# Layer 2's filler steps: from an even spread of a list to a fixed place in each attention unit

## The chip, the cores and the metric

The kernel runs on one core of one Trainium2 chip. The metric is the device time of one execution in microseconds (us); lower is better. A profile is one further execution, in which every instruction is recorded with its engine: TensorE (PE; its weight loads are PEld), VectorE (DVE), ScalarE (ACT), GpSimd (POOL) and SyncE (SP), which issues the DMAs.

## The reference

Four residual layers act in turn on an activation x of 4 images, 56 x 56 positions and 256 channels, all in float32:

```python
x = x + L0(_gn(x))   # 7x7 local attention, zero padded
x = x + L1(_gn(x))   # affinity over all 3136 positions of an image
x = x + L2(_gn(x))   # neighbourhood attention: 4 heads dense, 4 heads dilated by 2
x = x + L3(_gn(x))   # attention in shifted 7x7 windows
```

`_gn` normalises each group of 8 channels over the image. Only layer 2 is changed. It computes, per image,

```python
qkv = x @ w_qkv + b_qkv            # 256 -> 3 x 256, 8 heads of 32
attn = softmax(q @ k[window] + rpb)   # 7x7 window, clamped at the borders
out  = (attn @ v[window]) @ w_proj + b_proj
```

where heads 0 to 3 take their window with step 1 and heads 4 to 7 with step 2.

## The kernel before, in words

Channels lie on partitions (2 halves of 128), positions along the free dimension. Layer 2 goes through the images in chunks of 7 rows (392 positions, 32 chunks in all, numbered i), and attends in passes of 14 rows (16 passes, numbered r), in `stream`. One pass has 8 *units*, made by `pair(r, m, i)`: for each of four i first m = 0 (the dense heads) and then m = 1 (the dilated ones). So the even units, u0, u2, u4 and u6, are dense and the odd ones dilated.

`attend_pairs` runs over the units. For a unit it emits, in this order: the unit's logits (L1044, 32 matmuls into the PSUM tiles s0 and s1), the mask and exponentials (DVE L1051, ACT L1052 and L1054, POOL L1055), the sums of the two key pieces of the unit before (POOL L1064), the unit's *filler steps* (`w["fill"]`), then the products of the unit before (L1073, with v rows in `vp`, into ps_o), and its normalisation: a reciprocal (DVE L1598), a check sum of it (ACT L976, the tile `no`), and the multiply into the tile `attn` (DVE L1602, L1608).

The filler steps are other work of the layer that TensorE does between logits and products:

- `project_rows(i)` makes chunk i's values, keys and queries from its normalised rows `xn`, each in two halves, so six steps: v0, v1, k0, k1, q0, q1. A value step is 8 matmuls of 256 columns (L963) and a VectorE copy (L965). A key or query step is 4 matmuls of 392 columns (L946, in `project`) and ScalarE copies: four for keys (L1534; half 0 into kE and kI for the dense heads, half 1 into k2t for the dilated ones), one for queries (L1551). After v1 the values go to DRAM (L1529).
- `prepare(i)` normalises chunk i's rows on VectorE (L940) and then loads the chunk after it (L1493).
- `project_out(r - 1)` makes the output of the pass before: for each of two chunks two steps, here po0 to po3, each 4 matmuls (L946), the addition to the residual (DVE L1633) and its statistics (DVE L895). The first step of a chunk loads the residual (L1630), the second stores the result (L1636).
- `step_stats` does one of three steps that turn an image's statistics into the scale of the next normalisation, where one is pending: a VectorE aggregate, and two small matmuls, each followed by small VectorE (L914 to L918, L923) and GpSimd (L924, L926) instructions.

All projections write into two PSUM banks that take turns, `ps_m` (`m_bufs = 2`). v rows are gathered from DRAM when a unit's logits are emitted (L1592, tile `vp`, three buffers), by SP, whose queue runs in order.

Before, `stream` puts the pass's steps into one list (14 of chunks 2r + 3 and 2r + 4, with project_out after a quarter of it, and three statistics steps five places apart), and `spread` cuts that list into eight equal runs. For a full pass of 21 steps this gives, with ' for the second chunk:

| unit | steps |
|---|---|
| u0 | v0, v1 |
| u1 | k0, po0, po1 |
| u2 | po2, po3 |
| u3 | k1, statistics, q0 |
| u4 | q1, prepare, v0' |
| u5 | statistics, v1' |
| u6 | k0', k1', q0' |
| u7 | statistics, q1', prepare' |

Pass 0 has no output steps and no statistics steps, pass 14 one chunk only, pass 15 none. In layers 0 to 2 the framework's planner orders each engine's instructions: it goes by program order, but may take a later instruction that is ready first. In layer 3 the order is written out by hand. [...]two banks for ps_m, two for each of s0 and s1, two for ps_o.

Of the kernel before, what the change touches and what calls it, by code (L numbers as in the profile page):

```python
# [24 lines left out]
FP = mybir.dt.float32  # L25
# [10 lines left out]
P = 128  # L36
CC = C // P
# [59 lines left out]
WC2 = BT  # L97
# [734 lines left out]
def direct_blocks(ctx: ExitStack, tc: tile.TileContext, d: dict, watch):  # L832
# [7 lines left out]
    no_step = lambda: None  # L840
# [6 lines left out]
    def tokens_of(l, b, t0, n):  # L847
        return stream_of[l][b].rearrange("(h p) t -> p h t", p=P)[:, :, t0:t0 + n]
# [42 lines left out]
    def add_stats(l, b, i, x):  # L891

        if l < 4:
            for h in range(CC):
                nc.vector.bn_stats(out=raw[l][b][:, h, i, :], in_=x[:, h, :])  # L895
            seen_parts[l, b] = seen_parts.get((l, b), 0) + 1
            if seen_parts[l, b] == parts_of[l]:
                pending.extend(group_stats(l, b))
# [35 lines left out]
    def known(l, b):  # L934
        while (l, b) not in stats:
            pending.pop(0)()
        return stats[l, b]

    def normalise(dst, src, gst, h):
        nc.vector.tensor_scalar(dst, src, gst[:, h, 0:1], gst[:, h, 1:2], ALU.subtract, ALU.mult)  # L940

    def project(w, col, rhs, n):

        pm = ps_m()
        for h in range(CC):
            nc.tensor.matmul(pm[:, :n], lhsT=w[:, h, col:col + P], rhs=rhs(h),  # L946
                             start=(h == 0), stop=(h == CC - 1))
        return pm[:, :n]
# [144 lines left out]
    def spread(units, steps):  # L1093

        n = len(units)
        for i, w in enumerate(units):
            mine = steps[i * len(steps) // n:(i + 1) * len(steps) // n]
            w["fill"] = lambda mine=mine: [f() for f in mine]
            yield w

    def lazily(make, i, n):

        made = []
        return [lambda k=k: (made or made.extend(make(i)), made[k]()) for k in range(n)]
# [379 lines left out]
    def layer2(early, big, pool, brief):  # L1484
# [3 lines left out]
        xs, xns, q, attns = {}, {}, {}, {}  # L1488

        def load(i):  # L1490
            b, c = divmod(i, 2 * NSB)
            xs[i] = early.tile([P, CC, WC2], FP, tag="x", name="x2")
            nc.sync.dma_start(out=xs[i], in_=tokens_of(2, b, c * WC2, WC2))  # L1493
# [14 lines left out]
        def prepare(i):  # L1508
            b, c = divmod(i, 2 * NSB)
            x = xs.pop(i)  # L1510
            if i + 1 < NIMG * 2 * NSB:
                load(i + 1)
            xn = xns[i] = brief.tile([P, CC, WC2], FP, tag="xn", name="xn2")
            for h in range(CC):
                normalise(xn[:, h, :], x[:, h, :], known(2, b), h)
# [107 lines left out]
        def project_out(r):  # L1623
            b, g = divmod(r, NSB)

            def step(y, m, box={}):
                c = 2 * g + y
                if m == 0:
                    box["x"] = pool.tile([P, CC, WC2], FP, tag="xr", name="xr2")
                    nc.sync.dma_start(out=box["x"], in_=tokens_of(2, b, c * WC2, WC2))  # L1630
                x = box["x"]
                pm = project(w_p, m * P, lambda h: attns[r][:, h, y * WC2:(y + 1) * WC2], WC2)
                nc.vector.scalar_tensor_tensor(x[:, m, :], pm, bp2[:, m:m + 1], x[:, m, :], ALU.add, ALU.add)  # L1633
                if m:
                    add_stats(3, b, c, x)
                    nc.sync.dma_start(out=tokens_of(3, b, c * WC2, WC2), in_=x)  # L1636
            return [lambda m=m, y=y: step(y, m) for y in range(2) for m in range(CC)]

        def stream():
            n = NIMG * NSB  # L1640
            for r in range(n):
                steps = []
                for i in (2 * r + 3, 2 * r + 4):
                    if i < 2 * n:
                        steps += lazily(project_rows, i, 6)
                    if i + 1 < 2 * n:
                        steps.append(lambda i=i: prepare(i + 1))
                if r:
                    at = max(1, len(steps) // 4)
                    steps = steps or [no_step]  # L1650
                    steps[at:at] = project_out(r - 1)
                    for _ in range(3):
                        at = min(at + 5, len(steps))
                        steps.insert(at, step_stats)
                attns[r] = pool.tile([P, CC, 2 * WC2], FP, tag="attn", name="attn2")
                yield from spread([pair(r, m, i) for i in range(4) for m in range(2)], steps)

        prepare(0)
        for i in range(3):
            prepare(i + 1)  # L1660
            for step in project_rows(i):
                step()
        attend_pairs(pool, stream())
        for step in project_out(NIMG * NSB - 1):
            step()
# [304 lines left out]
```

## Time and profile before

| | |
|---|---|
| three runs | 4178.07, 4186.3, 4189.68 us |
| median | 4186.3 us |
| profiled execution | 4191.1 us from first to last instruction (4192.88 us device time) |
| busy, whole span | PE 95%, PEld 66%, DVE 57%, POOL 41%, ACT 32% |
| mean clock granted to TensorE | 0.975 |
| layer 2's passes | first logits at 2936.98 us, last output step ends near 3637 us |

In the page's rows by slice, each digit is a fortieth of the span (about 105 us) and gives the busy share in tenths, so that layer 2 is digits 28 to 34. In the list of waits, "A <- B" is the time in which engine and line A stood idle until B released it. In a timeline a line is a run of like instructions with its start and length, and in brackets the idle time before it.

### The profile page before, as it was taken

How to read it: one execution, taken by the hardware profiler on the slowest of the kernel's cores; microseconds unless marked ns; L12 is line 12 of the kernel's file. 1: busy time of each engine (PE TensorE's matmuls, PEld its weight loads, DVE VectorE, ACT ScalarE, POOL GpSimd, SP SyncE). 2: the span in 40 equal slices, each digit the busy share in tenths (PEclk: the TensorE clock that was granted, in tenths of full speed). 3: DMA queues.
4: the chain of work that ended last, by engine and by line, in shares of the span. 5: the costliest groups of instructions: out<-in, count | busy, mean ns of one | idle time of the engine just before them, and what ended most of it. 6: DMA issues, size and time to landing. Idle time of an engine off the chain costs nothing.

```text
span 4191.1 us, 92593 instructions
## 1 busy us (share of the span) xinstructions
PE 3978.8 (95%) x39191; PEld 2778.0 (66%) x39191; DVE 2380.0 (57%) x4437; ACT 1345.3 (32%) x2850; POOL 1738.4 (41%) x1883
## 2 busy tenths in 40 slices
PE   6899999799999999999999999998999999999998
PEld 4566666577777677776777767775666666666665
DVE  6777777633345433454334543445777777666665
ACT  2444445321111111121111111111554455444443
POOL 2566667611123211242112421123666666644444
PEclk9899999899999999999999999999999999999999
DMA  7344333310000100001000000001333343322221
GB/s 251 101 133 124 113 110 106 117 64 13 18 15 24 33 9 15 14 24 33 10 14 14 19 26 9 9 18 47 118 116 114 108 122 102 115 64 82 71 75 60
DMA packets 239794, 275.89 MB, mean 66 GB/s; under 512 B 22150, under 2 KB 231720, under 8 KB 238888
## 3 DMA queue, kind: packets, MB, share of 16 engines
q1 hardware_dynamic: 239082, 269.80, 20.7%
q8 instruction: 310, 5.08, 0.5%
q14 instruction: 114, 0.93, 0.1%
q10 hardware_dynamic: 288, 0.08, 0.0%
HBM read 190.29 MB, written 79.53 MB: 64 GB/s over the span
## 4 chain that ended last, share of the span: by engine, by line
PE 77%; DVE 12%; POOL 5%; issue 3%; ACT 2%; DMA 1%; SPq 0%; DVEq 0%; POOLq 0%; ACTq 0%
PE ps_m L946 15%; PE ps_o L1393 14%; PE ps_v L1385 11%; PE ps_s L1365 11%; PE ps_m L963 7%; PE ps_o L1073 5%; PE ps_s L1044 3%; PE ps_t L1380 3%; PE ps_o L1013 2%; DVE e L1051 2%; DVE rs L1598 1%; PE ps_s L998 1%; DVE rs L1218 1%; DVE xn L940 1%; PE ps_m L1329 1%
## 5 line engine op out<-in xcount | busy, mean ns | idle before, releaser
L1389 DVE TENSOR_TENSOR acc<-acc,ps_v 128x257 f32<-128x257 f32 x1104 | 459.5, 421 | 684.3 <-PE ps_v L1385 680.2
L1368 ACT ACTIVATE e<-ps_s 128x512 f32<-128x512 f32 (+3 forms) x364 | 200.7, 551 | 1465.9 <-PE ps_s L1365 1463.1
L1385 PE MATMUL ps_v<-xw,e 128*128 128x257 f32 x2400 | 638.8, 384 | 8.6 <-DVE acc L1389 8.6
L1393 PE MATMUL ps_o<-xw,at 128*128 128x257 f32 x2400 | 645.2, 391 | 0.5
L1365 PE MATMUL ps_s<-xnT,xd 128*128 128x512 f32 (+3 forms) x1456 | 630.2, 549 | 0.0
L1393 PEld LDWEIGHTS ps_o<-xw,at 128*128 128x128 f32 x2400 | 437.7, 190 | 131.7 <-ACT at L955 72.5
L1064 POOL TENSOR_TENSOR b<-e 126x336 f32<-126x336 f32 (+5 forms) x512 | 499.1, 995 | 15.7 <-ACT e L1052 7.5
L1385 PEld LDWEIGHTS ps_v<-xw,e 128*128 128x128 f32 x2400 | 423.8, 191 | 86.5 <-DVE acc L1389 27.8
L1361 POOL TENSOR_SCALAR xd<-xnT,vec 128x128 f32<-128x128 f32 x200 | 121.2, 617 | 786.9 <-PE ps_s L1365 780.5
L946 PE MATMUL ps_m<-xn,w_wqkv 128*128 128x392 f32 x1024 | 375.7, 505 | 25.8 <-ACT kE L1534 21.1
L1055 POOL TENSOR_TENSOR e<-e,m0t 126x672 f32<-126x672 f32 (+3 forms) x128 | 238.5, 1864 | 282.9 <-ACT e L1054 246.7
L1365 PEld LDWEIGHTS ps_s<-xnT,xd 128*128 128x128 f32 x1456 | 262.5, 190 | 139.8 <-issue 116.7
L1055 POOL TENSOR_TENSOR e<-e,bias 119x784 f32<-119x784 f32 (+5 forms) x128 | 244.2, 1908 | 236.5 <-ACT e L1054 236.1
L976 ACT ACTIVATE no<-rs 128x168 f32<-128x168 f32 (+2 forms) x256 | 93.8, 367 | 663.2 <-DVE rs L1598 323.9
L946 PEld LDWEIGHTS ps_m<-xn,w_wqkv 128*128 128x128 f32 x1024 | 186.4, 190 | 161.9 <-ACT kE L1534 31.0
L1073 PEld LDWEIGHTS ps_o<-e,vp 124*32 124x32 f32 (+3 forms) x8192 | 177.6, 111 | 138.0 <-issue 95.0
L1380 PEld LDWEIGHTS ps_t<-ident,e 128*128 128x128 f32 x1200 | 152.5, 142 | 143.9 <-issue 137.4
L1598 DVE RECIPROCAL rs<-ps_o 128x196 f32<-128x196 f32 (+2 forms) x128 | 176.3, 1377 | 124.6 <-PE ps_o L1073 124.5
L1073 PE MATMUL ps_o<-e,vp 124*32 124x112 f32 (+3 forms) x8192 | 240.4, 254 | 4.7 <-POOL e L1055 3.3
L963 PE MATMUL ps_m<-w_wqkv,xn 128*98 128x256 f32 x1024 | 243.6, 383 | 0.4 <-DVE xr L1440 0.4
L940 DVE TENSOR_SCALAR xn<-x,gst 128x28 f32<-128x28 f32 (+5 forms) x368 | 205.0, 612 | 40.8 <-PE ps_m L946 33.1
L1052 ACT ACTIVATE e<-e 126x672 f32<-126x672 f32 (+5 forms) x256 | 219.4, 857 | 25.3 <-DVE e L1051 11.8
(149 smaller groups left out, 6150.3 us busy)
## 6 DMA issues: line engine op xcount, KB each, us to landing
x<-xr SPq DMA_DIRECT2D x64, 392.0 KB
x<-in_x SPq DMA_DIRECT2D x53, 448.0 KB
x<-x SPq DMA_DIRECT2D x60, 392.0 KB
xr<-x SPq DMA_DIRECT2D x60, 392.0 KB
vd<-v SPq DMA_DIRECT2D x28, 448.0 KB
xr<-in_x SPq DMA_DIRECT2D x32, 392.0 KB
xr<-x SPq DMA_DIRECT2D x28, 448.0 KB
x<-xr SPq DMA_DIRECT2D x28, 448.0 KB
```

Of the source, the lines that this page charges most:

```text
L940: nc.vector.tensor_scalar(dst, src, gst[:, h, 0:1], gst[:, h, 1:2], ALU.subtract, ALU.mult)
L946: nc.tensor.matmul(pm[:, :n], lhsT=w[:, h, col:col + P], rhs=rhs(h), start=(h == 0), stop=(h == CC - 1))
L963: nc.tensor.matmul(pm[:n, j * C:(j + 1) * C], lhsT=xn[:, h, k * n:(k + 1) * n], rhs=w[:, h, :], start=(h == 0), stop=(h == CC - 1))
L1052: nc.scalar.activation(ev, ev, AF.Exp)
L1055: nc.gpsimd.tensor_tensor(parts(ev), parts(ev), w["emask"], ALU.mult)
L1064: nc.gpsimd.tensor_tensor(w["b"][a][:nk, :, :2 * nq].rearrange("p h (i c) -> p h i c", i=2), ev[:, :, :, 0, :], ev[:, :, :, 1, :], ALU.add)
L1073: nc.tensor.matmul(w["o"](k, i)[j * HD:(j + 1) * HD], lhsT=ones[:nk, :HD] if k else v(j, u), rhs=w["b"][j // 2][:nk, j % 2, i * nq:(i + 1) ...
L1365: nc.tensor.matmul(s[:, :n], lhsT=xd[j][:, h, :], rhs=xnT[:, h, first * P:last * P], start=(h == 0), stop=(h == CC - 1))
L1380: nc.tensor.transpose(pt[:, col(i)], e[:, col(i)], ident)
L1385: nc.tensor.matmul(pv[:, :C + 1], lhsT=e[:, col(i)], rhs=xw[:, j, :], start=True, stop=True)
L1389: nc.vector.tensor_tensor(acc[:, i, :], acc[:, i, :], pv[:, :C + 1], ALU.add)
L1393: nc.tensor.matmul(out[j][:, :C + 1], lhsT=e[:, col(i)] if i == j else at[:, col(i)], rhs=xw[:, i, :], start=(i == j), stop=(i == NB - 1))
```

## The change

Each unit of a pass is given its steps by number, in `work`, and `spread` is no longer used for this layer. For the two chunks (y = 0 and 1), unit 4y gets v0 and k0, unit 4y + 1 gets v1 and q0, unit 4y + 2 gets k1, unit 4y + 3 gets q1 and then the normalisation of the next chunk. The four output steps of the pass before go to the ends of u2, u3, u6 and u7, and the statistics steps to the ends of u1, u4 and u5 (in pass 0 too). The tile for the pass's result is taken before the steps are laid out.

| unit | steps |
|---|---|
| u0 | v0, k0 |
| u1 | v1, q0, statistics |
| u2 | k1, po0 |
| u3 | q1, prepare, po1 |
| u4 | v0', k0', statistics |
| u5 | v1', q0', statistics |
| u6 | k1', po2 |
| u7 | q1', prepare', po3 |

```diff
             for r in range(n):
-                steps = []
-                for i in (2 * r + 3, 2 * r + 4):
+                attns[r] = pool.tile([P, CC, 2 * WC2], FP, tag="attn", name="attn2")
+                work = [[] for _ in range(8)]
+                for y, i in enumerate((2 * r + 3, 2 * r + 4)):
                     if i < 2 * n:
-                        steps += lazily(project_rows, i, 6)
+                        v0, v1, k0, k1, q0, q1 = lazily(project_rows, i, 6)
+                        for a, steps in enumerate(((v0, k0), (v1, q0), (k1,), (q1,))):
+                            work[4 * y + a] += steps
                     if i + 1 < 2 * n:
-                        steps.append(lambda i=i: prepare(i + 1))
+                        work[4 * y + 3].append(lambda i=i: prepare(i + 1))
                 if r:
-                    at = max(1, len(steps) // 4)
-                    steps = steps or [no_step]
-                    steps[at:at] = project_out(r - 1)
-                    for _ in range(3):
-                        at = min(at + 5, len(steps))
-                        steps.insert(at, step_stats)
-                attns[r] = pool.tile([P, CC, 2 * WC2], FP, tag="attn", name="attn2")
-                yield from spread([pair(r, m, i) for i in range(4) for m in range(2)], steps)
+                    for u, step in zip((2, 3, 6, 7), project_out(r - 1)):
+                        work[u].append(step)
+                for u in (1, 4, 5):
+                    work[u].append(step_stats)
+                for u, w in enumerate(pair(r, m, i) for i in range(4) for m in range(2)):
+                    w["fill"] = lambda steps=work[u]: [f() for f in steps]
+                    yield w
```

## The prediction

> **What bounds the kernel now.** I read the page first: TensorE's busy share by slice, to see whether layer 2 (about 2937 to 3637 us) is limited by it.
>
> ```profile
> PE   6899999799999999999999999998999999999998
> PEclk9899999899999999999999999999999999999999
> ```
>
> TensorE is busy nine tenths or more of slices 28 to 34, at nearly full clock: what this layer can gain is TensorE's idle time. Next the waits between 2945 and 3600 us (total us, times, longest), which say what ended it:
>
> ```profile
> PE ps_m L946 <- ACT kE L1534: 33.1, 25, 3.0
> PE ps_m L946 <- DVE v L965: 4.7, 5, 3.2
> PE ps_s L1044 <- DVE e L1051: 0.8, 1, 0.8
> ```
>
> Nearly all of it is one wait: a projection's matmuls want one of the two ps_m banks while ScalarE (L1534, the copies of a key projection) or VectorE (L965, values) still empties it. 37.8 us in all. I then cut one pass of `stream` (r = 6) at the starts of its eight units' logits; columns are TensorE busy (matmuls), clock, DMA share, GB/s:
>
> ```profile
> 3204.68:3210.52 5.84, 5.84 (x101) 1.00 0.25 71
> 3210.52:3218.17 7.65, 6.72 (x97) 1.00 0.45 141
> 3218.17:3223.20 5.03, 5.03 (x92) 1.00 0.52 153
> 3223.20:3228.06 4.86, 4.86 (x92) 1.00 0.57 186
> 3228.06:3233.52 5.46, 5.46 (x97) 1.00 0.42 123
> 3233.52:3237.72 4.20, 4.20 (x92) 1.00 0.52 150
> 3237.72:3245.30 7.58, 6.62 (x97) 1.00 0.34 101
> 3245.30:3248.84 3.54, 3.54 (x89) 1.00 0.14 36
> sum 44.16, PE 42.28; mean PE 5.28
> ```
>
> Units last 3.5 to 7.6 us, and the two long ones (u1 and u6) hold the idle time: 0.93 and 0.96 us. They are the ones with three projections. The timeline of a u6 shows why (start, duration; TensorE here, ScalarE below):
>
> ```profile
> 3194.62 2.90 PE L946 MATMUL ps_m<-xn,w_wqkv 128*128 128x392 f32 x8
> 3198.47 1.58 PE L946 MATMUL ps_m<-xn,w_wqkv 128*128 128x392 f32 x4 [0.95 <-ACT kE L1534]
> ```
>
> ```profile
> 3195.82 0.71 ACT L1054 ACTIVATE e<-ps_s 126x672 f32<-126x672 f32 x1
> 3196.62 0.76 ACT L1052 ACTIVATE e<-e 126x672 f32<-126x672 f32 x1
> 3197.29 0.35 ACT L1534 ACTIVATE kE<-ps_m,vec 128x133 f32<-128x133 f32 x1
> ```
>
> The first key half is multiplied by about 3196.1, but ScalarE copies it only behind the unit's two exponentials (from 3197.29, over at 3198.4), and the third projection needs that bank.
>
> **What the Trainium skill says.** "Perfetto Trace Analysis", Matmuls: independent matmul groups should rotate through PSUM banks so that the evacuation of one overlaps the matmuls of the next. The trace agrees: two banks hide two projections in a unit (u2, u3, u4: no idle time), not three. The same page, Tensor Engine Instruction, calls ACT, DVE and GPSIMD strict FIFO; the copy queued behind the exponentials above fits that. "GPSIMD Engine Reference", Specifications, says that GpSimd shares its SBUF interfaces with VectorE. The trace fits here too: the pair of normalisations (L940) takes 0.88 us while GpSimd still has nothing to do (2937.09) and 2.65 us beside its multiply (3186.60).
>
> **The change part by part.** The matrix work is the same; steps move between units.
>
> *Two projections in every unit.* In steady passes each unit gets value + keys (u0, u4), value + queries (u1, u5), keys + output (u2, u6), queries + output (u3, u7). From rows of the table: u0 and u4 like the old u4 (5.46: one query and one value step with the same logits and products); u2 and u6 like the old u2 (5.03), u3 and u7 like the old u3 (4.86). u1 and u5: logits 1.02, fill 3.24 (in the old u4: 1.42 + 1.82), products 1.29: 5.55. Sum 2 x (5.46 + 5.55 + 5.03 + 4.86) = 41.80 against 44.16: -2.36, of which 1.89 is the two waits and 0.47 that a projection costs less in pairs (a lone one 1.51, two 2.83).
>
> *Does a wait remain?* Within a unit, with u3's start at 0: reciprocal and attn of the previous unit's held products to about 1.9, mask add to 2.9, ScalarE's exponentials to about 4.0, then the copy (queries 0.58, keys 1.1) to 4.5 or 5.1. The bank is wanted again by the same place of the next unit: at 6.1 or later in front of the logits' 1.05, later for the second place. Slack 1 us or more on each. The shortest: k1 (u2) is over at about 5.0, q1 wants its bank at 5.03 + 1.05 = 6.1. So I take no remaining wait.
>
> *Normalisations and output in u3 and u7.* VectorE there has add 0.96, normalisations 2.65, output 0.62, statistics 0.57, reciprocal 1.38, attn 0.36: 6.5 us in a unit of 4.86; the next unit has 3.5 us in 5.46. Together 10.0 in 10.3. It runs about 1.2 us late into u4, whose mask add then ends 1.2 us before u5's logits want the bank. Hidden, by TensorE's own 10.3 us.
>
> *Passes of shorter windows* (85 instead of 119 rows): in r = 3 the waits are 1.06 and 1.17 us, so 2.7 a pass. The layer has 13 full passes (r = 1 to 13), 7 at 2.36 and 6 at 2.71: 32.8 us.
>
> *Statistics.* The steps move to u1, u4, u5 and, as an image's last output step is now in u7, into the next pass (for layer 1's last image, into pass 0). Now each costs an extra 2.3 us at four places: the wait was 2.96 to 3.04 plus 0.27 to 0.42 instead of 0.95 to 1.17, because L916 to L918 hold VectorE for 1.84 + 0.80 + 0.80 us. In u4 the same chain delays u3's reciprocal by 3 us, and by the sums above u6's logits by some tenths. Bounds: all 9.2 us gained, or 4 x 1.5 lost if it meets a unit already late. I take 0.
>
> *DMAs.* SP's queue issues 40 gathers (0.72 us), two value stores, two loads of x, two of the residual and two output stores (0.37) a pass: 32 us of 41.8. The value store moves from u0 to u1 (first half), the output stores from u1 and u2 to u3 and u7; each holds the gathers behind it until VectorE has written. SP waits 74.8 us for products to free vp buffers, so it is ahead; TensorE's weight loads wait only 3.3 us for vp. Nothing taken; bounds 0 and +0.5 us a pass (+6). The residual's load is issued nearly a pass ahead (3221.34, used near 3257). On GpSimd only the statistics' 0.8 + 0.2 us move; its exponential products and sums fill 30.1 of 44.16 us, and would fill 72% after.
>
> *The last two passes.* Before, from 3587 us GpSimd is busy almost without a break (3.65 us a unit) and TensorE loses 6.6 us in all. The new empty units (u4, u5, then u0, u1, u4, u5) start that stretch earlier: 12 units x 3.65 = 43.8 + about 3 to fill, from u4 of r = 14, which starts 21.1 us into the pass instead of 18.6. 67.9 against 67.8: 0, at worst +3.
>
> *Not taken:* in pass 5 VectorE normalises rows of layer 3 in between, and TensorE waits 3.16 us; I expect the like elsewhere. The clock falls to 0.72 between 3140 and 3170, which costs some 5 us; kept (a bound of -5).
>
> Sum: -33 us on the span of 4191.1 (0.8%). That run took 4192.88, the others 4178.07 to 4189.68, median 4186.3. From the median: 4153.
>
> **Rivals.**
> (a) 72%: as above, 4153; its own range 4142 to 4168.
> (b) 13%: part comes back as another wait, at the same places. k1 now sits in u2 and u6, directly in front of logits that read k2t; if TensorE waits for the whole tile, or a gather behind the output store lands late, about 1 us returns at each of 26 places: 4179, no change. For: SP's load and the margin of a few tenths there. Against: ps_s never waits for L1534 before.
> (c) 9%: the order on the engines isn't the one written. The normalisation at 2937.09 runs three units before its step, so a planner reorders ready work; if it draws projections together again, half the gain goes: 4170. Against: TensorE's order in pass 6 is step for step the written one.
> (d) 6%: slower. VectorE becomes the bound in u3 and u7, as it has 10.0 us of work in 10.3. It decides once its mask add is over 1.2 us later than worked out. To end 0.3% above now, 26 places must lose (33 + 12.6) / 26 = 1.75 us each, so VectorE would have to be 3 us later: 4199. For: normalisation already triples beside GpSimd. Against: the old u4 held 6.2 us of VectorE work in 5.46, and u5 didn't wait.
>
> **How the numbers follow.** 0.3%, 12.6 us, is about what a measurement of this kernel can tell from no change. (a) is wholly faster; of (b) a third is, of (c) nearly all; the rest of both is the same, with some of (d). Faster 0.84, same 0.11, slower 0.05. The range: (a)'s lower end with the statistics' gain, 4140, up into (b), 4176.
>
> **What would show it.** The waits of L946 on L1534 fall from 33 us to under 5; a pass cut at its logits shows eight units of 4.9 to 5.6 us, none with idle time over 0.3, 41.8 in all; layer 3 starts some 33 us earlier and is unchanged. Wrong, if L1044 waits for L1534, L1051 or L1054 (b, d), L1073's weights for vp (b), or a unit still has three projections (c).

## The result, and the profile after

The changed kernel takes 4149.99 us in the median of 4 runs (4145.34 to 4155.33), the kernel before 4183.58 in 4 runs beside it (4178.07 to 4189.68). The ratio is 0.992, with a 95% interval from 0.99 to 0.9939: faster, by 33.6 us, which is less than 1% but clear of the noise. The forecast was 4153, between 4140 and 4176.

The page's rows by slice can't show the change: slices 28 to 34 (counted from 0) read 9 before and after, and a digit 9 takes in anything from 90% up. The list of waits (TensorE, 2945 to 3570 us) does show it:

```profile
PE ps_m L922 <- DVE v L965: 4.8, 4, 1.3
PE ps_o L1073 <- POOL b L1064: 1.9, 3, 0.7
PE ps_s L1044 <- DVE e L1051: 1.7, 2, 1.2
PE ps_m L913 <- DVE v L965: 1.3, 4, 0.5
...
PE ps_m L946 <- ACT k2t L1534: 0.7, 1, 0.7
```

The waits of L946 on L1534, 33.1 us before, are down to 0.7. What stands at the top now is the second small matmul of the statistics, L922, at its four places.

One steady pass (r = 2) cut at its eight units' logits; columns as in the prediction (length, TensorE busy, clock, DMA share, GB/s):

```profile
3014.20:3019.63 5.43, 5.43 (x97) 1.00 0.61 185
3019.63:3025.15 5.52, 5.52 (x96) 1.00 0.69 217
3025.15:3030.19 5.04, 5.04 (x93) 1.00 0.45 131
3030.19:3035.05 4.86, 4.86 (x93) 1.00 0.14 40
...
sum 41.69, PE 41.69; mean PE 5.21
```

In every unit, and in the sum, the first two numbers agree: TensorE has no idle time at all in this pass, and the units' lengths are the four of the prediction within 0.03 us (the second four repeat them within 0.01).

The timeline of u6 in that pass shows why, TensorE first and ScalarE below:

```profile
3047.05 1.58 PE L946 MATMUL ps_m<-xn,w_wqkv 128*128 128x392 f32 x4
3048.47 1.48 PE L946 MATMUL ps_m<-attn,w_wp 128*128 128x392 f32 x4
...
3051.04 1.09 PE L1044 MATMUL ps_s<-q,k2t 32*119 32x98 f32 x32
```

```profile
3048.25 0.71 ACT L1054 ACTIVATE e<-ps_s 126x672 f32<-126x672 f32 x1
3049.05 0.76 ACT L1052 ACTIVATE e<-e 126x672 f32<-126x672 f32 x1
3049.72 1.10 ACT L1534 ACTIVATE k2t<-ps_m,vec 128x136 f32<-128x136 f32 x4
```

ScalarE is no earlier than before: the key copy still stands behind the two exponentials, and starts at 3049.72, more than a microsecond after its matmuls. But nobody in this unit wants a third bank, and the copy is over at 3050.8, while the next unit's projection comes only after that unit's logits, at 3052.06.

A second measure is used below, because it is sharper than the time of the whole. The distance between the first dense logits of one pass and of the next gives the passes' lengths, and the sum from the first logits to layer 3's first projection gives layer 2. The code ahead of layer 2 is the same in all kernels here, and yet its first logits start anywhere from 2923.0 to 2938.4 us in the twelve profiles (the granted clock up to there was 0.976 in the earliest and 0.971 in the latest); layer 2 itself repeated to 0.1 us in two profiles of the changed kernel (664.04 and 664.13). From the traces, in us:

| part of layer 2 | before | after | change |
|---|---|---|---|
| regular pass, full windows | 44.16 | 41.69 | -2.47, 7 times |
| regular pass, shorter windows | 43.56 | 40.75 | -2.81, 6 times |
| pass 0 | 34.32 | 36.89 | +2.57 |
| above a regular pass, where one image's statistics are made: before in passes 1, 8 and 12, after in 9 and 13 | 2.99, 2.97, 2.92 | 2.19, 2.20 | -4.49 |
| above regular ones, passes 4 to 6: statistics, and layer 3's first rows are normalised | 10.79 | 6.70 | -4.1 |
| from pass 14 to layer 3 | 76.02 | 79.73 | +3.71 |
| layer 2 | 700.49 | 664.04 | -36.45 |

The regular passes give -34.1. The statistics of pass 1 before are those of pass 0 after, so its +2.57 belongs to the same account as the next row. Ahead of layer 2 the profiled run is 1.4 us shorter, and layer 3 is as it was (553.6 and 553.9 us). So the profiled executions differ by 37.6 us, 4191.1 to 4153.5.

### The profile page after: what moved, and what is told of

Its sections match the earlier page's. It is cut to its first block, busy times and chain, and to the rows that moved or that the text cites. A ratio compares the mean times of both kernels' runs of the same rounds, so it can differ in the third digit from the quotient of the medians.

```text
span 4153.5 us, 92576 instructions
## 1 busy us (share of the span) xinstructions
PE 3972.8 (96%) x39191; PEld 2781.3 (67%) x39191; DVE 2379.5 (57%) x4437; ACT 1347.9 (32%) x2850; POOL 1740.9 (42%) x1883
## 4 chain that ended last, share of the span: by engine, by line
PE 80%; DVE 11%; POOL 4%; issue 2%; DMA 1%; ACT 1%; SPq 0%; DVEq 0%; ACTq 0%; POOLq 0%
PE ps_m L946 17%; PE ps_o L1393 14%; PE ps_v L1385 12%; PE ps_s L1365 11%; PE ps_m L963 7%; PE ps_o L1073 5%; PE ps_s L1044 4%; PE ps_t L1380 3%; PE ps_o L1013 2%; DVE e L1051 1%; PE ps_s L998 1%; DVE rs L1218 1%; PE ps_m L1329 1%; DVE xn L940 1%; PE ps_m L1339 1%
## 5 line engine op out<-in xcount | busy, mean ns | idle before, releaser
L1064 POOL TENSOR_TENSOR b<-e 126x336 f32<-126x336 f32 (+5 forms) x512 | 499.6, 997 | 14.0 <-ACT e L1052 6.0
L946 PE MATMUL ps_m<-xn,w_wqkv 128*128 128x392 f32 x1024 | 376.6, 502 | 3.2 <-DVE xr L1633 2.5
L1055 POOL TENSOR_TENSOR e<-e,m0t 126x672 f32<-126x672 f32 (+3 forms) x128 | 238.9, 1867 | 282.6 <-ACT e L1054 245.5
L1055 POOL TENSOR_TENSOR e<-e,bias 119x784 f32<-119x784 f32 (+5 forms) x128 | 244.5, 1910 | 197.1 <-ACT e L1054 196.1
L946 PEld LDWEIGHTS ps_m<-xn,w_wqkv 128*128 128x128 f32 x1024 | 188.8, 190 | 125.3 <-ACT pr L1826 17.1
L1073 PEld LDWEIGHTS ps_o<-e,vp 124*32 124x32 f32 (+3 forms) x8192 | 176.9, 111 | 142.7 <-issue 94.0
L1073 PE MATMUL ps_o<-e,vp 124*32 124x112 f32 (+3 forms) x8192 | 240.2, 254 | 6.5 <-POOL e L1055 4.7
L940 DVE TENSOR_SCALAR xn<-x,gst 128x28 f32<-128x28 f32 (+5 forms) x368 | 206.2, 614 | 42.1 <-PE ps_m L946 31.6
```

The lines of the kernel that those rows point to most:

```text
L1055: nc.gpsimd.tensor_tensor(parts(ev), parts(ev), w["emask"], ALU.mult)
L1064: nc.gpsimd.tensor_tensor(w["b"][a][:nk, :, :2 * nq].rearrange("p h (i c) -> p h i c", i=2), ev[:, :, :, 0, :], ev[:, :, :, 1, :], ALU.add)
L1073: nc.tensor.matmul(w["o"](k, i)[j * HD:(j + 1) * HD], lhsT=ones[:nk, :HD] if k else v(j, u), rhs=w["b"][j // 2][:nk, j % 2, i * nq:(i + 1) ...
```

## The experiments

My theory at this point: two banks hide exactly two projections a unit, because a copy comes only behind the unit's other work on ScalarE or VectorE; two in every unit leave no wait, and a third waits about 1 us. (No run here gives ps_m a third bank, so that side of it is not tested.) Rivals: that it matters which steps share a unit (one half of the keys in a unit); that VectorE, loaded in u3 and u7, is close to being the bound. A pass below is a regular one with full windows, unless said; "layer 2" is the length in the trace.

**e1: two projections in every unit, in other pairs.** As far as may be those of the kernel before: u0 has v0 and v1, u1 k0 and po0, u2 po1 and po2, u3 k1 and q0, and u6 both halves of the second chunk's keys. u4 has q1 and v0', u5 v1' and po3, u7 q0' and q1'. Against the changed kernel:

```diff
-                        for a, steps in enumerate(((v0, k0), (v1, q0), (k1,), (q1,))):
-                            work[4 * y + a] += steps
+                        at = ((v0, 0), (v1, 0), (k0, 1), (k1, 3), (q0, 3), (q1, 4)) if y == 0 else \
+                            ((v0, 4), (v1, 5), (k0, 6), (k1, 6), (q0, 7), (q1, 7))
+                        for step, u in at:
+                            work[u].append(step)
...
-                        work[4 * y + 3].append(lambda i=i: prepare(i + 1))
+                        work[4 + 3 * y].append(lambda i=i: prepare(i + 1))
...
-                    for u, step in zip((2, 3, 6, 7), project_out(r - 1)):
+                    for u, step in zip((1, 2, 2, 5), project_out(r - 1)):
```

> Two projections in every unit, but both key halves of the second chunk together in u6, both query halves in u7, both value halves of the first chunk in u0, and two output steps in u2. If what counts is two projections a unit (two ps_m banks), no unit waits for a bank and the gain is that of the changed kernel: about 33 us faster than the kernel before (4150), a full pass of 41.7 us. If what counts is one half of the keys in a unit, u6 or u7 waits about 1 us a pass for L1534: some 13 us of the gain are lost (4163).

Measured: 4143.48 us, ratio to before 0.9899 (0.9882 to 0.9915); the pass is 41.75 us, layer 2 660.6. The timeline of TensorE, u6 and u7 of a pass:

```profile
3033.80 1.12 PE L1044 MATMUL ps_s<-q,kI 32*126 32x84 f32 x32
3034.85 2.90 PE L946 MATMUL ps_m<-xn,w_wqkv 128*128 128x392 f32 x8
...
3038.83 1.09 PE L1044 MATMUL ps_s<-q,k2t 32*119 32x98 f32 x32
3039.85 2.90 PE L946 MATMUL ps_m<-xn,w_wqkv 128*128 128x392 f32 x8
```

At 3034.85 eight key matmuls run as one group: both halves in one unit, with no idle time in front of them or in front of the queries after (3039.85). With these other pairs, and with units from 4.86 to 5.84 us, the gain is the same: what counts is how many steps share a unit, not which. The first rival falls. Layer 2 is even 3.4 us shorter than in the changed kernel, nearly all of it from pass 14 on (76.48 us instead of 79.73); e6 comes back to this.

**e2: a third projection put back in one place.** The second chunk's k0 moves from u4 to u6, where k1 and an output step are:

```diff
-                        for a, steps in enumerate(((v0, k0), (v1, q0), (k1,), (q1,))):
+                        for a, steps in enumerate(((v0, k0), (v1, q0), (k1,), (q1,)) if y == 0 else
+                                                  ((v0,), (v1, q0), (k0, k1), (q1,))):
```

> The changed kernel with one step moved back: the second chunk's first key half goes from u4 to u6, where it stands with the second half and an output step. Bank theory: in each of 14 passes with a second chunk the output step of u6 waits 0.9 to 1.2 us for L1534's copy of the first half, and u4 and u6 lose 0.1 by the regrouping: 14 to 18 us slower than the changed kernel, about 20 us faster than the kernel before (4165). If the even length of the units or the moved normalisation were the reason for the gain, almost nothing changes (4150).

Measured: 4178.11 us, ratio 0.9977 (0.9969 to 0.9986); the pass 42.91, +1.2. In the timeline of TensorE the wait is where it was put, and as long as before:

```profile
3045.53 2.90 PE L946 MATMUL ps_m<-xn,w_wqkv 128*128 128x392 f32 x8
3049.37 1.58 PE L946 MATMUL ps_m<-attn,w_wp 128*128 128x392 f32 x4 [0.95 <-ACT kE L1534]
```

In a regular pass, then, the whole expected loss: 0.95 of wait and 0.27 for two projections that run singly. But layer 2 is longer by 29.7 us, where 14 to 18 were expected, and ten passes without statistics at +0.7 to +1.7 account for only 13.6. The other 16.2 lie in the four passes with statistics, 2.5 to 5.8 us each. One part of them stands in the list of waits:

```profile
PE ps_m L922 <- DVE v L965: 12.3, 4, 3.4
```

L922 waits 3.1 us each time instead of 1.2. The traces of pass 9 in both kernels show where that comes from: L922 starts 5.37 us after VectorE's L917 (3335.98 and 3341.35 in the changed kernel, 3347.18 and 3352.55 here). So VectorE's work sets the time of L922, and the 1.4 us that u4 is shorter without its key step only lengthen the wait. I had not expected this. The other part is the granted clock. Passes 9 and 13 here, then pass 13 of the changed kernel (length, TensorE busy, clock, DMA share, GB/s):

```profile
3320.18:3366.58 46.40, 42.47 (x729) 1.00 0.39 115
3494.04:3543.70 49.66, 46.68 (x728) 0.90 0.30 91
```

```profile
3476.03:3519.92 43.89, 42.46 (x728) 1.00 0.33 102
```

In pass 13 the same matmuls keep TensorE busy 4.2 us longer, at a mean clock of 0.90. Over the four passes idle time makes up 7.6 us of the 16.2 and longer busy time 8.5 (at 0.92, 0.93 and 0.90 in passes 0, 5 and 13; none in pass 9). So e2 shows the price of a third projection in regular passes; its whole time overstates it.

**e3: the kernel before, with the dense heads' key copies on VectorE.** If ScalarE's queue is what makes the third projection wait, another engine's copy should end it in the old layout. Against the kernel before, in the copies of key half 0:

```diff
-                        act(dst[:, TR * c:TR * (c + 1), :], rows[:, :, c0:c0 + n])
+                        nc.vector.tensor_scalar(dst[:, TR * c:TR * (c + 1), :], rows[:, :, c0:c0 + n],
+                                                bk2[:, m:m + 1], None, ALU.add)
```

> The kernel before with its own layout; only the four copies of the first key half go from ScalarE to VectorE, where no exponential stands ahead of them. Bank theory: the bank of k0 is free before the third projection of u1 and u6 wants it; the waits for L1534 in u1 and u6 fall from 0.95 to about 0.2 us or less, a pass from 44.2 to about 42.5, 18 to 25 us faster than the kernel before (4160 to 4166). If the layout itself brings the gain (order and evenness of the units), the time stays at 4184, or rises by VectorE's 1 us more a half (4190).

Measured: 4171.23 us, ratio 0.9965 (0.9953 to 0.9978); a pass 42.73 instead of 44.16. The old u6, TensorE and then VectorE:

```profile
3049.59 2.90 PE L946 MATMUL ps_m<-xn,w_wqkv 128*128 128x392 f32 x8
3052.42 0.36 PE L1073 MATMUL ps_o<-e,vp 119*32 119x98 f32 x2
3052.74 1.55 PE L946 MATMUL ps_m<-xn,w_wqkv 128*128 128x392 f32 x4
```

```profile
3051.47 0.35 DVE L1539 TENSOR_SCALAR kE<-ps_m,vec 128x133 f32<-128x133 f32 x1
...
3052.24 0.35 DVE L1539 TENSOR_SCALAR kE<-ps_m,vec 128x133 f32<-128x133 f32 x1
```

VectorE has copied the first half 3.0 us after the projections began (3049.59 to 3052.59); ScalarE, behind its two exponentials, needed 3.8 (3194.62 to 3198.4 in the prediction's lines). The third projection starts 0.25 us after the second has ended, instead of 0.95, and two of the products' matmuls run in between. So what delays the copy decides, and not the number of banks by itself. No idle time of TensorE is left in the pass. Its busy time, 42.73, is 0.45 above the 42.28 of the prediction's table; two such places of 0.25 us would make that up. The last 0.6 from 42.28 down to 41.69 is what the prediction put down to pairs (0.47).

Layer 2 gains 13.7 us, or 16.9 from pass 1 on: in pass 0 two matmuls of the first logits run ahead of two projections, so that its count starts 3.2 us earlier. Pass 8, with statistics, gains nothing (46.55 against 46.53): its idle time falls by 2.1 us, from 4.5 to 2.4, but its busy time rises as much, at a granted clock of 0.96 where before it was 1.00.

**e4: normalisation done twice.** To measure how much room VectorE has in u3 and u7. The second one writes the same values again:

```diff
-                normalise(xn[:, h, :], x[:, h, :], known(2, b), h)
+                for _ in range(2):
+                    normalise(xn[:, h, :], x[:, h, :], known(2, b), h)
```

> The changed kernel with layer 2's normalisations done twice (the second writes the same values again): 0.9 to 2.6 us more VectorE work in u3 and u7. In the changed kernel's trace the mask add of u4 ends 1.5 us before the next logits want its bank. Theory: what goes beyond 1.5 us a place is lost, at 0.9 us the 26 full places give 23 us, so 0 to 29 us slower than the changed kernel (4150 to 4179). Rival, that VectorE already sets the pace in u3 and u7: the whole addition is lost, 26 x 2.4 = 63 us (4213). If it has wide slack: 0.

Measured: 4177.31 us, ratio 0.9974 (0.9966 to 0.9982); a pass 42.7 to 43.1, one with shorter windows 42.1 to 42.3, layer 2 691.0. VectorE's normalisation, and the waits on TensorE:

```profile
3070.60 4.44 DVE L940 TENSOR_SCALAR xn<-x,gst 128x392 f32<-128x392 f32 x4
```

```profile
PE ps_s L1044 <- DVE e L1051: 9.6, 25, 0.9
```

Two normalisations took 2.42 us and four take 4.44: 2.0 us more at each of two places in a pass. TensorE loses 1.0 to 1.6 a pass, so 0.5 to 0.8 a place: the first 1.2 to 1.5 us of the addition are hidden, and then the mask add of the next unit is late for the logits' banks, as rival (d) had it. In the changed kernel itself, the same place (VectorE, then TensorE):

```profile
3058.77 1.08 DVE L1051 TENSOR_TENSOR e<-ps_s,bias 124x896 f32<-124x896 f32 x1
```

```profile
3061.33 0.94 PE L1044 MATMUL ps_s<-q,k2t 32*85 32x98 f32 x32
```

The add ends at 3059.85, and the next logits start at 3061.33: 1.48 us of room. Both ways of measuring agree that VectorE has 1.2 to 1.5 us to spare here.

**The changed kernel again.** A second profile of it, beside the next three:

> The changed kernel once more, as the measure for the runs beside it: 4150 us, 33 us faster than the kernel before.

Measured: 4151.44 us, ratio 0.9913 (0.9897 to 0.9929); every pass as in the first profile to 0.05 us, layer 2 664.13.

**e5: the statistics steps at the ends of u1 and u2, and at the head of u6.** In the changed kernel the small matmuls are the third users of a bank in their unit. In pass 9 of the changed kernel, on TensorE:

```profile
3334.43 0.38 PE L913 MATMUL ps_m<-mv,group 128*128 128x2 f32 x2 [0.26 <-DVE v L965]
...
3341.35 0.38 PE L922 MATMUL ps_m<-dv,group 128*128 128x2 f32 x2 [1.16 <-DVE v L965]
```

The edit:

```diff
-                for u in (1, 4, 5):
-                    work[u].append(step_stats)
+                for u, at in ((1, 9), (2, 9), (6, 0)):
+                    work[u].insert(at, step_stats)
```

> The changed kernel with the statistics steps in u1, u2 and (first in the unit) u6 in place of the ends of u1, u4 and u5. In the changed kernel's trace passes 9 and 13 take 43.9 instead of 41.7 us: the second small matmul (L922) waits 1.15 us for the bank of v1', whose copy stands behind the small VectorE instructions L916 to L918. Theory: with the two small matmuls four units apart no bank is waited for, passes 9 and 13 fall to 42.2 to 42.7, and four places give 4 to 7 us (4144). Rival, that the 3.4 us of VectorE time itself is what costs: nothing gained (4150).

Measured: 4143.5 us, ratio 0.9897 (0.988 to 0.9913); pass 9 takes 43.77 instead of 43.88, where 42.2 to 42.7 were expected, and layer 2 664.0, unchanged. Up to pass 13 it gained 1.7 us, and it lost them again from pass 14 on (81.43 instead of 79.73). In the profiled runs, then, the lower time isn't from layer 2: its first logits start at 2924.5 instead of 2930.7. One wait went (L922, now at the head of u6, doesn't wait) and another came, on TensorE: the first small matmul is now third in u2.

```profile
3312.24 0.38 PE L913 MATMUL ps_m<-mv,group 128*128 128x2 f32 x2 [0.92 <-ACT k2t L1534]
```

0.92 us, what a third projection waits. Two columns of output take a bank like 392 do.

**e6: the last two passes' steps spread singly.** In the changed kernel the steps at the end (po3 in u7 of pass 15) leave this, on VectorE and on TensorE:

```profile
3593.59 1.28 DVE L1633 SCALAR_TENSOR_TENSOR xr<-ps_m,vec,xr 128x392 f32<-128x392 f32 x2 [1.38 <-PE ps_m L946]
3598.97 1.16 DVE L1633 SCALAR_TENSOR_TENSOR xr<-ps_m,vec,xr 128x392 f32<-128x392 f32 x2 [3.15 <-DMA xr<-x]
```

```profile
3589.63 7.54 PE L946 MATMUL ps_m<-attn,w_wp 128*128 128x392 f32 x16
3599.65 4.59 PE L946 MATMUL ps_m<-xn,w_wqkv 128*128 128x392 f32 x8 [2.48 <-DVE xr L1633]
```

The last chunk's output is multiplied by 3597.2, and VectorE stands idle for 3.15 us until the residual's load has landed; layer 3's first projection waits for the bank. The queue of SyncE shows why the load is late:

```profile
3581.19 0.42 SPq L1752 DMA_DIRECT2D m3l<-m3d  x1
3586.11 9.15 SPq L1636 DMA_DIRECT2D x<-xr  x2
3595.35 0.42 SPq L1630 DMA_DIRECT2D xr<-x  x1
```

Its buffer is the one that the output step in u7 uses. The store out of it is issued at 3586.11, behind a load of 2.4 MB for layer 3 (L1752), and by its semaphore in the trace it has landed only at 3594.49. The load follows at 3595.35, behind the next chunk's store (issued at 3594.90, merged into the second row), and lands at 3598.85. The edit gives pass 14's chunk one step a unit and takes the output steps of both passes earlier or further apart:

```diff
-                        for a, steps in enumerate(((v0, k0), (v1, q0), (k1,), (q1,))):
-                            work[4 * y + a] += steps
+                        if r < n - 2:
+                            places = (0, 1, 0, 2, 1, 3)
+                        else:
+                            places = (0, 1, 2, 3, 4, 5)
+                        for step, a in sorted(zip((v0, v1, k0, k1, q0, q1), places), key=lambda s: s[1]):
+                            work[4 * y + a].append(step)
...
-                    for u, step in zip((2, 3, 6, 7), project_out(r - 1)):
+                    for u, step in zip({n - 2: (3, 5, 6, 7), n - 1: (1, 2, 4, 6)}.get(r, (2, 3, 6, 7)), project_out(r - 1)):
```

> The changed kernel with the steps of the last two passes laid out singly: pass 14 v0, v1, k0, k1 + po0, q0, q1 + po1, po2, po3; pass 15 po0, po1, po2, po3 in u1, u2, u4, u6. In the changed kernel 79.7 us go by from pass 14's first logits to layer 3's first projection, 76.0 in the kernel before, with TensorE's own work about 69. Theory: GpSimd (3.65 us a unit) sets the pace where units are empty, and even filling lets TensorE and GpSimd run side by side over 16 units: 58.4 + 3 + about 10 at the end = 71 to 74, so 6 to 9 us faster than the changed kernel (4143). Rival, that the end (last units, last output steps) sets it: no gain.

Measured: 4145.32 us, ratio 0.9899 (0.9882 to 0.9915); all passes before the 14th as in the changed kernel, the stretch from pass 14 to layer 3 75.83 us instead of 79.73. The end on TensorE:

```profile
3593.16 5.54 PE L946 MATMUL ps_m<-attn,w_wp 128*128 128x392 f32 x12 [0.34 <-DVE attn L1602]
3598.53 2.80 PE L946 MATMUL ps_m<-xn,w_wqkv 128*128 128x392 f32 x8
```

Layer 3 starts with no wait: the store is issued at 3583.46 and has landed at 3587.83, and the load follows at 3587.88, now ahead of the 2.4 MB. The 3.9 us (6 to 9 were expected) make good the 3.7 that the change had cost, but the edit takes away two waits at once. From pass 14's first logits to the last products that wait for GpSimd's sums it is 67.6 us instead of 69.3 (67.8 before the change); from there to layer 3 it is 8.2 instead of 10.5 (8.2 before the change). So the load's wait is about 2.3 us of it, and the rest is that TensorE waits less for GpSimd (L1073 on L1055 and L1064: 3.5 us instead of 6.0, and 4.4 before the change). e1 separates the two by chance: its last output step is in u5, and no wait for the residual shows; it has 6.9 us in the second stretch and still 69.6 in the first.

**e7: e5 and e6 together.** No edit of its own.

> Both edits of the two runs before this one, steps of the statistics and of the last two passes. If the two are independent their gains add: 10 to 15 us faster than the changed kernel (4138).

Measured: 4143.05 us, ratio 0.9885 (0.9867 to 0.9904); layer 2 657.9 us, 6.2 less than in the changed kernel.

**e8: e6, with the small matmuls first in their units.** The first small step stays at u1's end, the second goes to the head of u2 and the third to that of u6: `((1, 9), (2, 0), (6, 0))` in e5's edit.

> The changed kernel with the last two passes laid out singly and the two small matmuls of the statistics as the first step of u2 and of u6 (the aggregate in u1). With the bank theory the third bank user is at the front, where its bank has long been free and its copy takes 0.15 us: passes 9 and 13 fall from 43.9 to about 42.5, layer 2 from 664 to about 655 us, 6 to 9 us faster than the changed kernel. If VectorE's time is what the statistics cost, passes 9 and 13 stay near 43.8 and layer 2 near 658.

Measured: 4140.04 us, ratio 0.9882 (0.9863 to 0.99); passes 9 and 13 43.24 us instead of 43.88 and layer 2 659.4, where 42.5 and 655 were expected. Its last two passes are longer than e6's (78.10 us against 75.83) at about the same idle time of TensorE: the granted clock in pass 15 was 0.85, in e6 0.88, in e7 0.92. The small matmuls themselves no longer wait; the projections behind them do, a little (0.8 us for L923 and as much for L914):

```profile
PE ps_m L946 <- DVE dv L923: 0.8, 3, 0.3
```

e8 and e7 have the two lowest medians of all, though e1's and e5's lie within 0.5 us of e7's. That they beat the kernel before is shown by their intervals; that they beat the changed kernel is shown by the length of layer 2 alone (657.9 and 659.4 against 664.0 and 664.1), as the intervals of the whole times overlap or touch.

**e9: the statistics left until the end.** Pass 5 of the changed kernel is 6.2 us longer than a regular one, and the like of passes 9 and 13 explains only 2.2 of that. The steps of images 0 to 2 are held back until pass 13; nothing is left out:

```diff
                 for u in (1, 4, 5):
-                    work[u].append(step_stats)
+                    if r == 0 or r > n - 4:
+                        work[u].append(step_stats)
```

> The changed kernel with the statistics for layer 3 left until passes 13 to 15 (one image a pass). In the changed kernel pass 5 takes 47.9 us, 6.2 more than its neighbours; there VectorE waits 3.1 us in front of layer 3's first normalisation for GpSimd's L924. If layer 3's early preparation is the cause, pass 5 falls to 41.7 and pass 9 to 41.7, and about 6 us turn up in pass 13 or 14; layer 2 within 5 us of 664. If pass 5 is long for another reason (the image border, the clock), it stays over 44.

Measured: 4147.57 us in its one run; pass 5 takes 41.70 us, pass 9 41.70, and pass 13 47.93; layer 2 is 667.6 us. What sits in pass 5 of the changed kernel, on VectorE and on GpSimd:

```profile
3170.17 0.16 DVE L923 TENSOR_SCALAR dv<-ps_m 128x2 f32<-128x2 f32 x1 [0.48 <-PE ps_m L922]
3173.40 1.47 DVE L940 TENSOR_SCALAR xn<-x,gst 128x343 f32<-128x343 f32 x5 [3.07 <-POOL gst L924]
```

```profile
3169.16 1.86 POOL L1055 TENSOR_TENSOR e<-e,bias 119x784 f32<-119x784 f32 x1 [2.65 <-ACT e L1054]
3170.98 1.71 POOL L1064 TENSOR_TENSOR b<-e 119x392 f32<-119x392 f32 x2
3172.65 0.71 POOL L924 TENSOR_TENSOR gst<-dv,mhalf 128x2 f32<-128x2 f32 x1
```

and in pass 13 of e9, on VectorE:

```profile
3490.60 1.47 DVE L940 TENSOR_SCALAR xn<-x,gst 128x343 f32<-128x343 f32 x5 [3.08 <-POOL gst L924]
```

When the first image's statistics are done, the planner puts layer 3's first normalisation of 343 positions next on VectorE. It needs L924's result, which GpSimd gives only behind two long instructions (1.86 and 1.71 us), so VectorE stands idle for 3.07 us with the attention's work queued behind it. The same wait, 3.08, moves with the statistics to pass 13. It belongs to the hand-over to layer 3, and not to the layout of the steps.

## Why the prediction was right

Step by step, as the prediction has them.

- **The bound.** Right. The waits of L946 on L1534 were most of what layer 2 could gain; without them a steady pass has no idle time on TensorE.
- **Two projections in every unit.** Right to 0.11 us a pass: 41.69 for 41.80. The wait that went is the 1.9 us foretold; TensorE's busy time fell from 42.28 to 41.70 where 0.47 was foretold, so pairs cost a little less than assumed. Thirteen passes gave 34.1 us, 32.8 were foretold. e2 shows the price of a third in a regular pass, e1 that other pairs do as well.
- **No wait remains.** Right in steady passes. k1's copy was over at 3050.8 in a unit that began at 3046.00: 4.8 us in, for the 5.0 worked out.
- **Normalisations in u3 and u7.** Right: 1.48 us of room for the 1.2 worked out, and e4 finds 1.2 to 1.5. Rival (d) needed VectorE to be 3 us later; its mechanism is real and begins where it was put, but the change doesn't come near.
- **Statistics.** Taken as 0, with bounds of -9.2 and +6. Of the four places three can be compared one by one (pass 1 to 0, 8 to 9, 12 to 13): -0.4, -0.8 and -0.7, so -1.9 (the first of these as far as the new layout adds nothing else to pass 0). The number is near, but the prediction didn't count the small matmuls as users of a bank. A small matmul at the end of a unit that has two projections is a third user of a bank and waits 1.2 us; behind it stands the chain of small VectorE instructions that I had named (L917 to L922 in e2). That the old wait went and a smaller one came is in part luck.
- **Not taken.** Passes 4 to 6 lost 10.8 us above regular ones and lose 6.7 now. Layer 3's normalisation is there again, as expected (3.07 us). The clock of before was 0.50 for two stretches of 6.8 us, near two idle times of TensorE (from 3147.3 and 3164.4); after, for one of 3.4 us (from 3180.0). TensorE's busy time above that of regular passes fell from 6.3 to 2.8 us and its idle time from 4.5 to 3.9, so 3.5 of the 4.1 us go with the clock, inside the bound of -5. Why the clock falls isn't settled: in e9 pass 13 has more idle time, and a clock of 1.00 in it and for 26 us behind it.
- **DMAs in steady passes.** Right: TensorE's weight loads wait 6.7 us for vp rows in the whole layer (3.3 before), and no steady pass is longer for it.
- **The last two passes.** The step that failed, by 3.7 us where 0, at worst +3, was taken. Two terms were too small. The stretch that GpSimd paces was worked out as 67.9 against 67.8 before; measured from the same start to the last products that wait for its sums, it is 69.3: it begins where foretold (20.9 us into pass 14 for 21.1), but the twelve units and the filling take 48.4 us and not 46.8. And the residual's load was counted as issued nearly a pass ahead, from a steady pass. In the last pass its buffer is held by the output step that the change puts in u7, and the store out of it lands only at 3594.49; TensorE waits 2.48 us for what follows. In e6 both are back (67.6 us, and no such wait), and the end is as long as before (75.83 and 76.02 us). That the late landing comes from the 2.4 MB issued ahead of the store is how the trace reads (8.4 us from issue to landing, 4.4 in e6, where the 2.4 MB come later); no edit moved that load alone.

The sum was -33 us for the span; it was -37.6 in the profiled executions and -33.6 in the medians. Regular passes -34.1, statistics -1.9, passes 4 to 6 -4.1, the end +3.7 make layer 2's -36.45. That the last two, which the prediction took as 0, nearly cancel is luck.

Rival (b), a wait that comes back: its place (k1 in front of logits that read k2t, the gathers behind the output store) shows 0.7 us in one instance on L1534 in the whole layer. Rival (c): TensorE's order in the regular passes was the one written. Both fall.

## What to carry to other kernels

Where groups of matmuls rotate through few banks, count the groups between two points at which the copies catch up. With two banks, two were free here, and each one more waited for what stood queued in front of the copy, however small the group was; other numbers of banks were not run. A layout worked out for steady passes has to be gone through once more for the first and the last one, where a buffer that is refilled "a pass ahead" may not be free in time, and where other transfers, here those of the next layer, stand in the same queue. When only one layer changes, compare that layer's length in the traces before the whole time: here it repeated to 0.1 us in two profiles of one kernel, while what runs ahead of it varied by 15. Then split the difference into idle and busy time of the engine, since a lower granted clock lengthens only the second (e2, e3, e8).

## What was not expected of the hardware

*A small VectorE instruction on two operands in SBUF lasts as long as the GpSimd instruction that it meets.* In the changed kernel's pass 9, VectorE and then GpSimd:

```profile
3334.85 0.16 DVE L914 COPY gst<-ps_m 128x2 f32<-128x2 f32 x1 [0.48 <-PE ps_m L913]
3335.04 0.90 DVE L916 TENSOR_TENSOR dv<-mv,gst 128x2 f32<-128x2 f32 x1
```

```profile
3333.82 2.11 POOL L1055 TENSOR_TENSOR e<-e,bias 124x896 f32<-124x896 f32 x1 [2.09 <-ACT e L1054]
```

L916 ends at 3335.94, GpSimd's multiply at 3335.93. L917 and L918 take 1.06 and 1.05 us and end at 3337.04 and 3338.13, each 0.02 us behind one of GpSimd's two sums (3337.02 and 3338.11). So it is with all 119 instructions of these three lines, in layer 2 of the twelve profiles, that start while a GpSimd instruction runs: they end 0.01 to 0.02 us after it. L914 has its one operand in PSUM and takes 0.16 us beside the same multiply, and L923 likewise (3170.17 in e9's lines). In e5 GpSimd's sums end at 3313.85 and nothing follows until 3316.70:

```profile
3313.90 0.16 DVE L917 TENSOR_TENSOR dv<-dv 128x2 f32<-128x2 f32 x1
...
3315.28 0.10 DVE L918 TENSOR_TENSOR dv<-dv,mv 128x2 f32<-128x2 f32 x1
```

The normalisation pair is slowed too (0.88 us alone, 2.42 to 2.65 beside GpSimd). "GPSIMD Engine Reference" of the Trainium skill, Specifications, says that GpSimd's SBUF interfaces are shared with VectorE, with contention among others for VectorE instructions "with two SBUF inputs". The trace agrees, and shows how long the wait is here: the rest of GpSimd's instruction, so that 128 x 2 elements take up to 2.05 us.

*The granted clock falls in stretches of one length.* In layer 2 of all twelve profiles it is either 1.00 or 0.50, and 0.50 for 3.41 us or a multiple of it: 6.8 us twice in the kernel before, 3.4 in pass 5 of the changed kernel, 10.2 in pass 13 of e2. These stretches lie near idle times of TensorE, but not near every one: of e2's four waits for L922, of 3.0 to 3.4 us, those in passes 0, 5 and 13 have one and that in pass 9 has none. What decides is not settled here.
